# A scan over the running decay product, one add-and-clip per step, with matmuls on quadrants of TensorE

## The chip, the cores and the metric

The kernel runs on one core of a Trainium2 chip. Its time is the device time of a run in microseconds, from the first to the last instruction on the core, and the figure quoted is the median of several runs. Everything is computed in float32.

The engines that matter here are TensorE (PE, with its weight loads as PEld), VectorE (DVE), ScalarE (ACT) and GpSimd (POOL). Each works through its own queue in order and waits for the others by semaphores.

## The reference

The input x has 32 sequences of 256 tokens with 256 channels. A state-space block comes first, then two layers of local attention and a gated feed-forward network, and x is added at the end. The change touches the state-space block alone. Its core, cut to what matters:

```python
xn = layernorm(silu(conv(x @ W_in.T + cond)))            # [b, t, 512]
Bm, Cm, dt = split(xn @ W_xproj.T, 3)                    # 16 states each
Ad = 1.0 - 0.01 * tanh(dt @ W_dt.T + b_dt) * tanh(A_log) # decay, [b, t, 16]
Bd = Bm * min(norm(xn), 1)

def step(h, (ad, bd, xt, ct)):                           # h: [b, 16, 512]
    h = clip(h * ad[:, :, None] + bd[:, :, None] * xt[:, None, :], -10, 10)
    return h, einsum('bd,bdh->bh', ct, h)                # y of this step

y = scan(step, 0) + D * xn
out = (y * silu(gate)) @ W_out.T
```

A step depends on the state that the step before it left, and the clip keeps the recurrence from being written as one linear scan.

## The kernel before

Eight sequences are scanned together (a group; there are four groups). The state h is one tile of 128 partitions, 8 sequences times 16 states, by 512 channels. Time runs in 16 blocks of 16 steps; 8 sequences times 16 steps are the 128 token rows of a block. A group goes through the convolution, the scan, and two layers of attention and feed-forward; nothing of one group overlaps much with the next.

The inner loop, with two matmuls on TensorE and two operations on VectorE in each step:

```python
nxt = prep(0)
for tb in range(NTB):                       # 16 blocks
    xn, lbs, ct, ad, sg = nxt
    if tb + 1 < NTB:
        nxt = prep(tb + 1)                  # for the next block
    y = ps_y.tile([P, DI], FP, ...)
    for t in range(TB):                     # 16 steps
        h, s = divmod(t, TH)
        if s == 0:
            put_c(h, ct)
        bx = ps_bx.tile([P, DI], FP, ...)   # Bd * x of this step
        nc.tensor.matmul(bx, lbs[h][:, s * P : (s + 1) * P], xn, start=True, stop=True)
        h_new = hp.tile([P, DI], FP, ...)
        nc.vector.scalar_tensor_tensor(     # h * ad + bx
            h_new, h_old, ad[:, t : t + 1], bx, ALU.mult, ALU.add)
        nc.vector.tensor_scalar(h_new, h_new, -CLIP, CLIP, ALU.max, ALU.min)
        nc.tensor.matmul(y, ly[h][:, s * P : (s + 1) * P], h_new,
                         start=(t == 0), stop=(t == TB - 1))
        h_old = h_new
    z = sp.tile([P, DI], FP, ...)
    nc.gpsimd.tensor_mul(z, xn, dskip_sb)
    nc.vector.tensor_add(z, z, y)
    nc.gpsimd.tensor_mul(z, z, sg)
    ...                                     # 4 transposes to tz, ACT copies them to zT;
    ...                                     # every fourth block W_out: 8 matmuls to po
```

The weights of the first matmul, `lb`, are 128 by 128 for each step, zero but for the eight rows of that step, so only 8 of its 128 rows contribute. The weights of the second, `ly`, hold C of that step in the eight columns of its tokens.

What `prep` does for the next block, in order, shortened to the operations and their engines:

```python
def prep(tb):
    # PE    4 transposes of xc -> tp_x
    # DVE   bn_stats, bn_aggr, + eps; POOL ** -0.5; DVE xn = (tp_x - mean) * rstd
    # POOL  xn *= lng, xn += lnb
    # ACT   sum of squares -> ss; DVE sc = min(ss, 1); POOL nrm = sc ** 0.5
    # PE    4 transposes -> tp_xn; ACT copies them to xnT
    # PE    pp = xnT @ W_xproj.T; DVE copies it to pr
    # PE    pd = transpose of dt; DVE dT; PE pd2 = dT @ W_dt
    # DVE   da = pd2 + b_dt; ACT tanh; DVE * a_row
    bd = ...                                # DVE, 128 x 16
    for h in range(2):                      # lb: 2 x [128, 1024] on POOL
        nc.gpsimd.tensor_mul(lb, bc(ident_tb[:, h * TH : (h + 1) * TH, :], 3, NS),
                             bc(bc(bd, 1, GB), 1, TH))
    # DVE   wide (twice); PE pc = C and dt * A by (sequence, state) rows
    nc.vector.tensor_copy(ct, pc[:, 0:TB])
    nc.vector.tensor_scalar_add(ad, pc[:, TB : 2 * TB], 1.0)
    # POOL  xt; PE gp = xt @ W_in (gate), 2 matmuls; ACT sg = silu(gp)
    return xn, lbs, ct, ad, sg

def put_c(h, ct):                           # DVE, into the diagonal of ly
    nc.vector.tensor_mul(diag, bc(ct[:, h * TH : (h + 1) * TH], 2, GB), bc(of_seq, 1, TH))
```

Of the kernel before, what the change touches and what calls it, by code (L numbers as in the profile page):

```python
# [7 lines left out]

FP = mybir.dt.float32
AF = mybir.ActivationFunctionType  # L10
# [4 lines left out]
P = 128  # L15
S = 256          # tokens of a sequence
DM = 256         # model width
KM = DM // P
DI = 512         # inner width of the state-space block
NC_ = DI // P  # L20
NS = 16          # states per channel
GB = 8           # sequences scanned together: GB * NS = 128 partitions
TB = P // GB     # time steps of a token tile: GB * TB = 128 partitions
NTB = S // TB
TH = TB // 2
# [3 lines left out]
W = 128          # attention window  # L29
# [8 lines left out]
def bc(ap, axis, n):  # L38
    """ap with a new axis of n equal entries (stride 0)."""
    ap = ap.unsqueeze(axis)  # L40
    shape = list(ap.shape)
    shape[axis] = n
    return ap.broadcast_to(shape)
# [3 lines left out]
def kernel(  # L47
    ctx: ExitStack,
    tc: tile.TileContext,
    xT,        # [P, KM, B, S]      x, channel-major  # L50
    condT,     # [P, NC_, B]
    w_inT,     # [P, KM, 2 * DI]
    w_conv,    # [P, NC_, TAPS]
    b_conv,    # [P, NC_]
    s_ln_g,    # [DI]
    s_ln_b,    # [DI]
    w_xT,      # [P, NC_, 3 * NS]
    w_dtT,     # [NS, NS]
    b_dt,      # [NS]
    a_log,     # [NS]  # L60
    d_skip,    # [DI]
    w_outT,    # [P, NC_, DM]
    wqkv,      # [P, L, KM, 3 * DI]
    qk_scale,  # [L, 2, DH]
    qk_scale_sw,  # [L, 2, DH]      the halves of a head swapped
    wo,        # [P, L, NC_, DM]
    f_ln_g,    # [P, L, KM]
    f_ln_b,    # [P, L, KM]
    w1,        # [P, L, KM, 2 * HID]
    b1,        # [P, L, 2, len(MCH)]  # L70
    w2,        # [P, L, len(MCH), DM]
    b2,        # [P, L, KM]
    rot_c,     # [P, NW, 2, DH]     rotary tables of positions
    rot_s,     # [P, NW, 2, DH]
    outT,      # [P, KM, B, S]
):
# [44 lines left out]
    # Token tiles have partition b * TB + t; the scan has partition b * NS + n.  # L121
    # of_seq[p, b] = (p // TB == b), of_step[p, t] = (p % TB == t)
    of_seq = const.tile([P, GB], FP, tag="of_seq", name="of_seq")
    nc.vector.tensor_reduce(of_seq, ident.rearrange("p (b t) -> p b t", b=GB), AX.X, ALU.add)
    of_step = const.tile([P, TB], FP, tag="of_step", name="of_step")
    nc.vector.tensor_reduce(of_step, ident.rearrange("p (b t) -> p t b", b=GB), AX.X, ALU.add)
    ident_tb = ident.rearrange("p (b t) -> p t b", b=GB)
# [6 lines left out]
    # 0.01 * A, A = -tanh(A_log)  # L134
# [4 lines left out]
    # Additive mask of a window's queries over the window before it and itself.  # L139
# [11 lines left out]
    # Rotary tables with the layer's q and k scales in them.  # L151
# [18 lines left out]
    # Transposed weights of the state read-out, two half tiles: zero but where the step is.  # L170
    ly = []
    for i in range(2):
        t = const.tile([P, TH * (P + 1)], FP, tag=f"ly{i}", name=f"ly{i}")
        nc.gpsimd.memset(t, 0.0)
        ly.append(t)

    def rsqrt(pool, src, n, name):
        """src ** -0.5, [P, n]."""
        r = pool.tile([P, n], FP, tag=f"{name}_r", name=f"{name}_r")
        nc.gpsimd.tensor_tensor(r, src, neg_half[:, 0:n], ALU.pow)  # L180
        return r

    def group_scan(g, xg, res):
        """x -> y of the state-space block, into res (channel-major, column 0 of each
        sequence zero)."""
        with ExitStack() as es:
            xcp = es.enter_context(tc.tile_pool(name=f"xc{g}", bufs=1, reuse_waits="tile"))
            # token tiles side by side: [channel, block of steps, sequence, step]
            xc = xcp.tile([P, NC_, NTB, GB, TB], FP, tag="xc", name=f"xc_{g}")

            with tc.tile_pool(name=f"cv{g}", bufs=2, reuse_waits="tile") as cv, tc.tile_pool(
                name=f"cvp{g}", bufs=4, space=PSUM, reuse_waits="tile"
            ) as cvp:
                for j in range(GB // 2):
                    for c in range(NC_):
# [22 lines left out]
                        for k in range(1, TAPS):  # L218
# [4 lines left out]
                        nc.scalar.activation(  # L223
                            xc[:, c, :, 2 * j : 2 * j + 2, :].rearrange("p n b t -> p b n t"),
                            acc.rearrange("p b (n t) -> p b n t", n=NTB),
                            AF.Silu,
                        )

            sp = es.enter_context(tc.tile_pool(name=f"sp{g}", bufs=2, reuse_waits="tile"))
            hp = es.enter_context(tc.tile_pool(name=f"hp{g}", bufs=3, reuse_waits="tile"))  # L230
# [3 lines left out]
                tc.tile_pool(name=f"pbx{g}", bufs=3, space=PSUM, reuse_waits="tile")  # L234
            )
            ps_y = es.enter_context(
                tc.tile_pool(name=f"py{g}", bufs=2, space=PSUM, reuse_waits="tile")
# [8 lines left out]
            def prep(tb):  # L246
                """What the scan of a block of steps needs."""
                ts_ = slice(tb * TB, (tb + 1) * TB)
                tp = ps_t.tile([P, DI], FP, tag="tp", name="tp_x")
                for c in range(NC_):  # L250
                    nc.tensor.transpose(
                        tp[:, c * P : (c + 1) * P],
                        xc[:, c, tb].rearrange("p b t -> p (b t)"),
                        ident,
                    )
# [14 lines left out]
                # min(|xn|, 1)  # L270
# [35 lines left out]
                bd = sm.tile([P, NS], FP, tag="bd", name="bd")  # L306
                nc.vector.tensor_scalar_mul(bd, pr[:, 0:NS], nrm)
                # lb[(b, t), t', b', n] = Bd[(b, t), n] where t' = t and b' = b
                lbs = []
                for h in range(2):  # L310
                    lb = sp.tile([P, TH, GB, NS], FP, tag="lb", name="lb", bufs=3)
                    nc.gpsimd.tensor_mul(  # L312
                        lb,
                        bc(ident_tb[:, h * TH : (h + 1) * TH, :], 3, NS),
                        bc(bc(bd, 1, GB), 1, TH),
                    )
                    lbs.append(lb.rearrange("p t b n -> p (t b n)"))

                # C and dt * A from rows (b, t) to rows (b, n)
                wide = sm.tile([P, 2, GB, NS], FP, tag="wide", name="wide", bufs=1)  # L320
                nc.vector.tensor_mul(
                    wide[:, 0], bc(of_seq, 2, NS), bc(pr[:, NS : 2 * NS], 1, GB)
                )
                nc.vector.tensor_mul(wide[:, 1], bc(of_seq, 2, NS), bc(da, 1, GB))
                pc = ps_s.tile([P, DI], FP, tag="pss", name="pc")
                for i in range(2):
# [3 lines left out]
                        of_step,  # L330
# [3 lines left out]
                ct = sm.tile([P, TB], FP, tag="ct", name="ct")  # L334
                nc.vector.tensor_copy(ct, pc[:, 0:TB])
                ad = sm.tile([P, TB], FP, tag="ad", name="ad")
                nc.vector.tensor_scalar_add(ad, pc[:, TB : 2 * TB], 1.0)

                # silu(gate)
                xt = sm.tile([P, KM, GB, TB], FP, tag="xt", name="xt", bufs=2)  # L340
                nc.gpsimd.tensor_copy(xt, xg[:, :, :, ts_])
                gp = ps_t.tile([P, DI], FP, tag="tp", name="gp")
                for k in range(KM):
                    nc.tensor.matmul(  # L344
                        gp, xt[:, k].rearrange("p b t -> p (b t)"), w_in_sb[:, k, DI : 2 * DI],
# [4 lines left out]
                return xn, lbs, ct, ad, sg  # L350

            def put_c(h, ct):
                """ly[(b, n), s, (b', t')] = C[(b, n), t'] where t' = h * TH + s and b' = b"""
                diag = ly[h].rearrange("p (s r) -> p s r", r=P + 1)[
                    :, :, h * TH : h * TH + (GB - 1) * TB + 1 : TB
                ]
                nc.vector.tensor_mul(
                    diag, bc(ct[:, h * TH : (h + 1) * TH], 2, GB), bc(of_seq, 1, TH)
                )

            zT = None
            h_old = hp.tile([P, DI], FP, tag="h", name="h0")
            nc.vector.memset(h_old, 0.0)
            nxt = prep(0)
            for tb in range(NTB):
                xn, lbs, ct, ad, sg = nxt
                if tb + 1 < NTB:
                    nxt = prep(tb + 1)
                y = ps_y.tile([P, DI], FP, tag="y", name="y")
                for t in range(TB):  # L370
                    h, s = divmod(t, TH)
                    if s == 0:
                        put_c(h, ct)
                    bx = ps_bx.tile([P, DI], FP, tag="bx", name="bx")
                    nc.tensor.matmul(  # L375
                        bx, lbs[h][:, s * P : (s + 1) * P], xn, start=True, stop=True
                    )
                    h_new = hp.tile([P, DI], FP, tag="h", name="h")
                    nc.vector.scalar_tensor_tensor(  # L379
                        h_new, h_old, ad[:, t : t + 1], bx, ALU.mult, ALU.add  # L380
                    )
                    nc.vector.tensor_scalar(h_new, h_new, -CLIP, CLIP, ALU.max, ALU.min)  # L382
                    nc.tensor.matmul(  # L383
                        y, ly[h][:, s * P : (s + 1) * P], h_new,
                        start=(t == 0), stop=(t == TB - 1),
                    )
                    h_old = h_new

                # (y + D * xn) * silu(gate), then W_out
# [10 lines left out]
                if q == 0:  # L400
                    zT = zp.tile([P, NC_, 4, P], FP, tag="zT", name="zT")
                nc.scalar.copy(zT[:, :, q, :], tz.rearrange("p (c t) -> p c t", c=NC_))  # L402
# [376 lines left out]
```

## Time and profile before

Three runs took 7459.3, 7441.64 and 7459.2 us, median 7459.2. The profiled run:

| what | value |
|---|---|
| span | 7442.3 us |
| PE busy | 6294.6 us (85%) |
| PE weight loads | 3214.0 us (43%) |
| DVE busy | 3504.5 us (47%) |
| ACT busy | 1552.8 us (21%) |
| POOL busy | 1871.4 us (25%) |
| mean TensorE clock granted | 0.874 |

A group of instructions on the page is read so: source line, engine, operation, output and inputs, shape and count; then busy time in us and the mean of one in ns; then the idle time of the engine just before these instructions, and what ended it. PE busy times overlap at the ends of matmuls, so that starts, not durations, tell the rate. A line of the timeline gives the start, the duration, the engine, the source line, what was done and how often, and in brackets how long the engine had been idle and for whom.

### The profile page before, as it was taken

To read this page: it belongs to the slowest core of one execution; us is meant where nothing else is said; L and a number is where in the kernel's file an instruction comes from. 1 tells how busy PE (TensorE), PEld (TensorE's weight loads), DVE (VectorE), ACT (ScalarE), POOL (GpSimd) and SP (SyncE) were. 2 spreads that over 40 slices of the span, in tenths; PEclk is the share of its full clock that TensorE was granted. 3 is DMA by queue.
4 is the path that set the end of the run, shared out by engine and by line. 5 is a ranking of instruction groups with operands and counts; after the bars stand their busy time and mean duration, and the time that the engine had idled before them with its cause. 6 is when DMAs were issued, how large, how long until landed. Compare 5 with 4: busy or idle time off the path is not lost. (4 is left out here: it accounts for less than half of the span.)

```text
span 7442.3 us, 55547 instructions
## 1 busy us (share of the span) xinstructions
PE 6294.6 (85%) x19648; PEld 3214.0 (43%) x19648; DVE 3504.5 (47%) x6691; ACT 1552.8 (21%) x4066; POOL 1871.4 (25%) x1649
## 2 busy tenths in 40 slices
PE   6989888888799988888879898888887899888888
PEld 2444553553344455355334445535533444553553
DVE  5666442442566644244256664424425666442442
ACT  1000331331100033133110003313311000331331
POOL 3222330330322233033032223303303222330331
PEclk8999888888899988888889998888888999888888
DMA  2000000000000000000000000000000000000000
GB/s 74 0 0 12 1 1 0 1 6 14 3 0 0 12 1 1 0 1 6 15 3 0 0 12 1 1 0 1 6 16 2 1 0 0 1 0 0 1 6 17
DMA packets 14021, 40.37 MB, mean 5 GB/s; under 512 B 2352, under 2 KB 3376, under 8 KB 12080
## 3 DMA queue, kind: packets, MB, share of 16 engines
q1 hardware_dynamic: 10832, 34.78, 1.3%
q8 instruction: 156, 2.56, 0.1%
q10 hardware_dynamic: 2912, 2.05, 0.1%
q14 instruction: 121, 0.99, 0.0%
HBM read 28.43 MB, written 8.39 MB: 5 GB/s over the span
## 5 line engine op out<-in xcount | busy, mean ns | idle before, releaser
L383 PE MATMUL y<-h,ly 128*128 128x512 f32 x2048 | 1088.4, 616 | 83.4 <-DVE h L382 83.4
L375 PE MATMUL bx<-xn,lb 128*128 128x512 f32 x2048 | 1019.0, 596 | 3.0 <-POOL lb L312 3.0
L379 DVE SCALAR_TENSOR_TENSOR h<-h,ad,bx 128x512 f32<-128x512 f32 x1024 | 764.8, 747 | 392.8 <-PE bx L375 368.9
L180 POOL TENSOR_TENSOR ss_r<-ss,neg_half 128x8 f32<-128x8 f32 x256 | 420.2, 1641 | 1783.0 <-DVE ss L464 1773.7
L447 PE MATMUL ps_qkv<-wqkv_sb,res 128*128 128x512 f32 x1536 | 730.2, 597 | 0.0
L383 PEld LDWEIGHTS y<-h,ly 128*128 128x128 f32 x2048 | 375.7, 196 | 535.2 <-DVE h L382 420.2
L503 PE MATMUL sc<-kT,qT 64*128 64x128 f32 (+1 forms) x2048 | 578.3, 425 | 27.0 <-ACT kT L485 27.0
L375 PEld LDWEIGHTS bx<-xn,lb 128*128 128x128 f32 x2048 | 381.6, 190 | 445.6 <-issue 442.2
L382 DVE TENSOR_SCALAR h<-h 128x512 f32<-128x512 f32 x1024 | 557.9, 545 | 29.1
L511 DVE TENSOR_TENSOR p_sb<-sc,mask 128x512 f32<-128x512 f32 x384 | 257.7, 682 | 584.6 <-PE sc L503 433.6
L533 PEld LDWEIGHTS ov<-v_sb,pT 128*128 128x128 f32 x3072 | 479.1, 240 | 110.5 <-issue 41.5
L533 PE MATMUL ov<-v_sb,pT 128*128 128x64 f32 x3072 | 503.9, 326 | 8.8 <-DVE pT L530 7.1
L519 ACT ACTIVATE p_sb<-p_sb,nmax 128x128 f32<-128x128 f32 (+1 forms) x1024 | 453.5, 445 | 202.2 <-DVE nmax L515 198.4
L480 PE MATMUL tr_qk<-ident,rot 128*128 128x128 f32 x1024 | 181.7, 304 | 369.0 <-POOL rot L477 362.1
L624 PE MATMUL pg<-hT,w_sb 128*128 128x512 f32 (+1 forms) x768 | 420.9, 676 | 7.3 <-ACT hT L610 4.4
L635 DVE SCALAR_TENSOR_TENSOR ag<-pa,b_sb,gl 128x512 f32<-128x512 f32 x192 | 143.9, 750 | 577.5 <-PE pa L624 562.1
L402 ACT COPY zT<-tz 128x512 f32<-128x512 f32 x64 | 37.5, 585 | 1704.5 <-PE tz L396 1704.5
L180 POOL TENSOR_TENSOR ve_r<-ve,neg_half 128x1 f32<-128x1 f32 x192 | 105.5, 549 | 1135.5 <-DVE ve L599 1005.6
L312 POOL TENSOR_TENSOR lb<-ident,bd 128x1024 f32<-128x1024 f32 x128 | 258.0, 2017 | 522.5 <-PE bx L375 329.4
L503 PEld LDWEIGHTS sc<-kT,qT 64*128 64x128 f32 x2048 | 303.7, 219 | 191.5 <-ACT kT L485 90.2
L393 POOL TENSOR_TENSOR z<-z,sg 128x512 f32<-128x512 f32 x64 | 80.9, 1265 | 1170.2 <-DVE z L392 1170.2
L624 PE MATMUL pa<-hT,w_sb 128*128 128x512 f32 (+1 forms) x768 | 366.3, 599 | 0.0
(122 smaller groups left out, 8025.4 us busy)
## 6 DMA issues: line engine op xcount, KB each, us to landing
xg<-in_xT_dram SPq DMA_DIRECT2D x8, 1024.0 KB, 6.6
xs<-in_xT_dram SPq DMA_DIRECT2D x16, 512.0 KB, 4.0
out_dram<-fo SPq DMA_DIRECT2D x32, 256.0 KB, 2.0
wqkv_sb<-in_wqkv_dram SPq DMA_DIRECT2D x1, 3072.0 KB, 12.2
w_sb<-in_w_dram SPq DMA_DIRECT2D x1, 2728.0 KB, 12.2
w_sb<-in_w_dram SPq DMA_DIRECT2D x1, 1536.0 KB, 16.0
w_in_sb<-in_w_inT_dram SPq DMA_DIRECT2D x1, 1024.0 KB, 5.1
wo_sb<-in_wo_dram SPq DMA_DIRECT2D x1, 1024.0 KB, 4.9
```

Source lines behind the costliest of these rows:

```text
L180: nc.gpsimd.tensor_tensor(r, src, neg_half[:, 0:n], ALU.pow)
L312: nc.gpsimd.tensor_mul(lb, bc(ident_tb[:, h * TH : (h + 1) * TH, :], 3, NS), bc(bc(bd, 1, GB), 1, TH),)
L375: nc.tensor.matmul(bx, lbs[h][:, s * P : (s + 1) * P], xn, start=True, stop=True)
L379: nc.vector.scalar_tensor_tensor(h_new, h_old, ad[:, t : t + 1], bx, ALU.mult, ALU.add)
L382: nc.vector.tensor_scalar(h_new, h_new, -CLIP, CLIP, ALU.max, ALU.min)
L383: nc.tensor.matmul(y, ly[h][:, s * P : (s + 1) * P], h_new, start=(t == 0), stop=(t == TB - 1),)
L447: nc.tensor.matmul(ps, res[:, k, b, t0 : t0 + W], wqkv_sb[:, l, k, a * DI : (a + 1) * DI], start=(k == 0), stop=(k == KM - 1),)
L503: nc.tensor.matmul(sc[:, i, :], qT[rows, h0 + i, w * W : (w + 1) * W], kT[rows, h0 + i, k0 : k0 + nk], start=True, stop=True,)
L511: nc.vector.tensor_add(p_sb, sc, bc(mask[:, 2 * W - nk :], 1, nh))
L519: nc.scalar.activation(p_sb[:, i, :], p_sb[:, i, :], AF.Exp, bias=nmax[:, h : h + 1], accum_out=rsum[:, h : h + 1],)
L533: nc.tensor.matmul(ov[:, h, :], pT[:, i, kb * W : (kb + 1) * W], v_sb[:, k0 // W + kb, h * DH : (h + 1) * DH], start=(kb == 0), stop=(kb = ...
L624: nc.tensor.matmul(ps[0:n, :], w1_sb[:, l, k, half_ * HID + o : half_ * HID + o + n], hT[:, k].rearrange("p b t -> p (b t)"), start=(k == ...
```

## The change

With p[t] the product of all decays up to step t, the state over it, g = h / p, follows g[t] = clip(g[t-1] + (Bd x)[t] / p[t], -10 / p[t], 10 / p[t]). The multiplication by the decay leaves the inner loop: Bd is divided by p and C multiplied by p when a block is prepared, the limits become one value for each row and step, and add and clip can be one instruction of VectorE, a custom operation `TENSOR_ADD_SAT` (in0 + in1, then min with s0 and max with s1).

The tokens of a block are put in another order, (q, i, b) with step 4 i + q, so that a step's eight rows lie within one of four strips of 32 rows. The first matmul of a step then takes 32 rows of weights and of xn instead of 128, and the second writes 32 output rows instead of 128 (32 columns of weights). Four steps in turn use the four strips; each bx strip has a PSUM bank of its own.

What it is for: half the VectorE instructions in a step, and matmuls that need a quarter of the array, which four of them might share. The diff, cut to its core:

```diff
-            def prep(tb):
+            def prep(tb, p_old):
 ...
-                bd = sm.tile([P, NS], FP, tag="bd", name="bd")
-                nc.vector.tensor_scalar_mul(bd, pr[:, 0:NS], nrm)
-                lbs = []
-                for h in range(2):
-                    lb = sp.tile([P, TH, GB, NS], FP, tag="lb", name="lb", bufs=3)
-                    nc.gpsimd.tensor_mul(lb, ...)
 ...
-                nc.vector.tensor_copy(ct, pc[:, 0:TB])
                 nc.vector.tensor_scalar_add(ad, pc[:, TB : 2 * TB], 1.0)
+                nc.vector.tensor_tensor_scan(pd_, ad, zero_tb, p_old, ALU.mult, ALU.add)
+                nc.vector.reciprocal(pi, pd_)
+                nc.gpsimd.tensor_scalar_mul(lim[:, 0], pi, CLIP)
+                nc.gpsimd.tensor_scalar_mul(lim[:, 1], pi, -CLIP)
+                nc.vector.tensor_mul(ct, pc[:, 0:TB], pd_)
+                nc.gpsimd.tensor_mul(piw, ...)                # 128 x 128
+                nc.tensor.matmul(pp2[:, 0:NS], piw..., st_n, start=True, stop=True)
+                nc.vector.scalar_tensor_tensor(               # Bd / p
+                    bd, pr[:, 0:NS], nrm, pp2[:, 0:NS], ALU.mult, ALU.mult)
+                lb = sp.tile([P, NI * GB, NS], FP, tag="lb", name="lb", bufs=2)
+                nc.gpsimd.tensor_mul(lb, bc(tok_row, 2, NS), bc(bd, 1, NI * GB))
 ...
-                nc.vector.tensor_mul(                         # put_c
-                    diag, bc(ct[:, h * TH : (h + 1) * TH], 2, GB), bc(of_seq, 1, TH)
-                )
+                nc.gpsimd.tensor_mul(                         # put_c, once a block
+                    diag, bc(ct..., 3, GB), bc(bc(st_seq, 1, NQ), 1, NI))
 ...
+                put_c(lyt, ct)
-                for t in range(TB):
-                    ...                                       # the loop shown above
+                for i in range(NI):                           # 4 rounds
+                    hs = []
+                    for q in range(NQ):                       # of 4 steps
+                        t = i * NQ + q
+                        rows = slice(32 * q, 32 * q + 32)
+                        bx = ps_bx.tile([P, DI], FP, tag=f"bx{q}", name=f"bx{q}")
+                        nc.tensor.matmul(
+                            bx, lb[rows, i * GB : (i + 1) * GB, :]..., xn[rows, :],
+                            start=True, stop=True)
+                        h_new = hp.tile([P, DI], FP, tag="h", name="h")
+                        nc.vector._custom_dve(
+                            TENSOR_ADD_SAT, out=h_new, in0=h_old, in1=bx,
+                            s0=lim[:, 0, t : t + 1], s1=lim[:, 1, t : t + 1])
+                        hs.append(h_new)
+                        h_old = h_new
+                    for q in range(NQ):
+                        t = i * NQ + q
+                        nc.tensor.matmul(
+                            y[32 * q : 32 * q + 32, :], lyt[:, 32 * t : 32 * t + 32],
+                            hs[q], start=(i == 0), stop=(i == NI - 1))
```

Cut here: comments, the constants, the new order of tokens in xc, xt (two copies on POOL in place of one) and in the copies of the output, and the SiLU after the convolution, which becomes two instructions of 256 elements in place of one of 512. The buffers of h grow from 3 to 8; bx has four banks with one buffer each in place of three buffers; y has one buffer in place of two.

## The prediction

> **What bounds the kernel now.** I read four views in this order: the page's slices and groups (where the time is), the busy time by stretch (what the scan is worth), the timeline of one block of 16 steps (what waits for what), and the order of both programs' instructions on each engine. First the page: the rows of slices (tenths busy, and the clock), and the groups of the scan.
>
> ```profile
> PE   6989888888799988888879898888887899888888
> DVE  5666442442566644244256664424425666442442
> PEclk8999888888899988888889998888888999888888
> ...
> L383 PE MATMUL y<-h,ly 128*128 128x512 f32 x2048 | 1088.4, 616 | 83.4 <-DVE h L382 83.4
> L375 PE MATMUL bx<-xn,lb 128*128 128x512 f32 x2048 | 1019.0, 596 | 3.0 <-POOL lb L312 3.0
> L379 DVE SCALAR_TENSOR_TENSOR h<-h,ad,bx 128x512 f32<-128x512 f32 x1024 | 764.8, 747 | 392.8 <-PE bx L375 368.9
> ...
> L382 DVE TENSOR_SCALAR h<-h 128x512 f32<-128x512 f32 x1024 | 557.9, 545 | 29.1
> ```
>
> The pattern repeats four times (four groups of 8 sequences); the "666" and the clock digits "999" mark the scan. One f32 matmul leaves two records (2048 for 1024), so one step costs TensorE two matmuls and VectorE two operations. Two of the four scans by stretch:
>
> ```profile
> 1930.00:2600.00 670.00, 603.52 (x1580) 278.61 (x1581) 409.78 (x785) 47.76 (x104) 170.25 (x144) 0.94 0.01 4
> ...
> 5645.00:6315.00 670.00, 604.82 (x1583) 279.22 (x1584) 409.74 (x785) 48.34 (x105) 169.39 (x142) 0.94 0.00 0
> ```
>
> The columns are length, then busy time of PE, PE loads, DVE, ACT, POOL, then clock. A scan takes about 670 us, so the four take 2680 of 7442 us; PE is busy 90% of it, DVE 61%. The steady part of a block (timeline of PE, then of DVE):
>
> ```profile
> 5939.56 1.02 PE L375 MATMUL bx<-xn,lb 128*128 128x512 f32 x2
> 5940.42 1.02 PE L383 MATMUL y<-h,ly 128*128 128x512 f32 x2
> 5941.28 1.02 PE L375 MATMUL bx<-xn,lb 128*128 128x512 f32 x2
> ```
>
> ```profile
> 5938.91 0.75 DVE L379 SCALAR_TENSOR_TENSOR h<-h,ad,bx 128x512 f32<-128x512 f32 x1 [0.51 <-PE bx L375]
> 5939.69 0.43 DVE L382 TENSOR_SCALAR h<-h 128x512 f32<-128x512 f32 x1
> 5940.62 0.75 DVE L379 SCALAR_TENSOR_TENSOR h<-h,ad,bx 128x512 f32<-128x512 f32 x1 [0.51 <-PE bx L375]
> ```
>
> Starts of matmuls are 0.86 us apart without a gap; DVE idles 0.51 us in each step for bx. The step is 1.72 us, all TensorE: 16 steps are 27.5 us. Yet blocks follow each other every 41.8 us (the DVE clip that waits behind POOL recurs at 5756.81, 5797.99, 5842.59 and 5883.51). The other 14 us come from preparing the next block, whose chain is threaded into the same queues:
>
> ```profile
> 5952.12 0.75 PE L280 MATMUL tp_xn<-ident,xn 128*128 128x128 f32 x4 [1.98 <-POOL xn L268]
> 5952.87 2.08 PE L344 MATMUL gp<-w_in_sb,xt 128*128 128x512 f32 x2
> ...
> 5956.56 0.21 DVE L293 COPY pr<-pp 128x48 f32<-128x48 f32 x1 [2.37 <-PE pp L288]
> ...
> 5958.61 0.28 DVE L298 COPY dT<-pd 16x128 f32<-16x128 f32 x1 [1.17 <-PE pd L296]
> ...
> 5960.25 0.17 DVE L302 TENSOR_TENSOR da<-pd,bdt_sb 128x16 f32<-128x16 f32 x1 [1.36 <-PE pd L300]
> ```
>
> PE idles 1.98 us for POOL's layer norm, then DVE waits in turn for pp, pd, pd and pc; from 5952 to 5963 only one step is added. The stretch 5952 to 5963 has a clock of 0.69, so its matmuls are slower (gp: 2.08 us for two records).
>
> [...] idle time of 1.98 us is followed by the clock of 0.69. [...] the clip L382 takes 0.43 us alone and 1.97 us while POOL writes lb (2.02 us).
>
> **The change, part by part.**
> - *VectorE.* Multiply-add (0.75) and clip (0.43) become one add with limits. It has L379's shape and one PSUM input, so I give it 0.75, 0.78 from start to start. A block's 16 steps: 12.5 us in place of 18.9. The plain clip was what stalled behind POOL, so some 1.5 us a block of that go too. New: scan, reciprocal, both on 128x16, about 0.25 each, partly for ct's copy. put_c (two of 0.60) goes to POOL. DVE was not the bound, so none of this counts by itself.
> - *POOL.* lb shrinks from two of 2.02 us to one 128x512, about 1.1; limits, piw and put_c add about 1.5. Hidden, but piw now lies between DVE's reciprocal and PE's pp2.
> - *TensorE.* The same 32 matmuls a block, each still 512 columns and two records of 0.43, now on quadrants. [...] I do not expect four in the time of one, but a new matmul each 0.43 us: (4+1) x 0.43 = 2.15 us for four in place of 3.44.
> - *Order.* The built program's PE order in a steady round of four steps is y0 y1 y2, next bx0, y3, next bx1 bx2 bx3. y takes column strips and bx row strips of the whole array[...].
>
> A steady round, from the end of the last add (0): y2 ends 0.08, bx0 runs 0.18 to 1.04, y3 1.1 to 2.0, bx1 2.1 to 2.96; 0.2 us later (3.2) DVE starts three adds of 0.78 and ends at 5.5. bx2 and bx3 come 0.43 apart and are in time. So 5.5 us for four steps (1.38 a step) against 6.9.
>
> One whole block by the built order: round 0 ends its adds at 5.5; z (0.68, then POOL 1.27) lets PE transpose at 4.3, tp_x ends at 5.4. Four y to 7.6, four bx to 9.9. Meanwhile st to xn on DVE end at 8.3 and POOL's two xn at 11.1; round 1 adds until 11.1, the last after sc at 12.9. tp_xn, ACT, gp, pp, gp at half clock: pr at 15.5, gp to 17.1, pd, dT 17.8, one y, pd2, da, tanh, wide 20.4. The other y and bx0 let round 2 start at 22.2; with bx1 to bx3 it ends at 26.3. Reciprocal 26.6, POOL's lim and piw 27.3, pp2 at 27.4 in front of y3: y3 to 28.4, bx1 29.4, adds 29.6 to 31.9. So 32 us against 41.0; the W_out product (6.95 us, every fourth block) now sits in front of the remaining y, adding about 1.3 a block on average, against 0.8 now. 33.3 against 41.8 is 8.5 saved, x 64 blocks = 544 us.
> - *Convolution.* SiLU in two halves costs ACT about 0.3 more per tile of 64; the chain there is POOL and DVE, so at most part shows: +12 us.
> - Sum: 7459 - 544 + 12 = 6927.
>
> **Rivals.**
> - *No concurrency in f32.* 64-row score matmuls exist already, but consecutive ones share their rows, so the trace says nothing. Then 32 x 0.86 = 27.5 + about 6.5 of preparation at full clock + 1.5 idle + 1 to 2 of switches = 37: still better than 41.8, as eight matmuls now stand in front of tp_xn and cover POOL's latency. Time 7459 - 64 x 4.8 = about 7150.
> - *Half clock.* If quarter-used strips count as little activity, or the new waits (pp2, tp_xn) idle PE too long, bx0, y3 and bx1 take 1.72 each: 7.9 us a round and about 47 us a block, 7800. [...] Against: in the steady round PE has hardly a gap.
> - *Full concurrency.* Four in 0.86 us: the round stays at 5.5, since the three dependent matmuls y2/bx0, y3, bx1 and three adds are the chain; only the bursts shrink, to about 31 a block: 6800.
> - *A slow custom add.* 0.25 us more each is about 0.75 a round, 3 a block: 7120.
>
> **Range and chances.** The main path gives 6927, full concurrency 6800, no concurrency 7150, half clock 7800. I lean a little upwards, to 6960, range 6700 to 7320. Faster by over 2% (under 7310): 0.84; within: 0.08; slower: 0.08, nearly all of it the half clock.
>
> **What would show it.** The groups bx and y keep 2048 records each; their starts in a burst 0.43 apart confirm half overlap, 0.86 none, under 0.25 full. The new add near 0.75, and DVE's idle time moving to waits for bx after y3, in a stretch of about 540 us per scan; POOL's 1.97 stalls gone; attention unchanged. A scan clock well under 0.9, or adds over 0.9 us, would prove me wrong.

## The result, and the profile after

The changed kernel takes 7242.7 us (median of 4 runs, 7238.7 to 7244.4) against 7459.3 before: a ratio of 0.972, with a 95% interval of 0.971 to 0.974. It is faster, by 217 us, where 499 were expected.

First the page of the changed kernel: its rows of slices, and the groups of the scan (out<-in, partitions x elements, count | busy us, mean ns of one | idle time of the engine before them, and its releaser).

```profile
PE   6988888888788888888878888888887888888888
DVE  4444442442444444244244444424424444442442
PEclk8778878888877887888888788798887778879878
...
L421 DVE CUSTOM_DVE_ANT_0 h<-h,bx,lim 128x512 f32<-128x512 f32 x1024 | 825.4, 806 | 759.9 <-PE bx L413 705.3
L429 PE MATMUL y<-h,ly 128*32 128x512 f32 x2048 | 857.1, 766 | 10.6 <-DVE h L421 10.6
L413 PE MATMUL bx<-xn,lb 32*128 32x512 f32 x2048 | 733.2, 782 | 0.0
```

VectorE has fallen to 4 tenths in the scans, as meant, and now waits for bx (705 of its 760 us of idle time at this line). But the clock digits of the scans have gone from 9 to 7 and 8, and a record of y or bx shows 770 ns on average where it showed 600, although each matmul uses a quarter of the array. The same in one window of the second group, from the z of its first block to the z of its last (length, then busy time of PE, PE loads, DVE, ACT, POOL, then the clock):

```profile
1944.00:2492.00 548.00, 484.04 (x1474) 153.97 (x1472) 256.19 (x479) 41.97 (x91) 131.78 (x184) 0.78 0.01 4
```

TensorE is busy for 88% of it, much as before, at a clock of 0.78 in place of 0.94. The timeline of TensorE shows a stretch of a block at half clock (0.50 from 5605.0 to 5611.4), and after it one at full clock (1.00 from 5614.5 to 5625.0):

```profile
5605.05 2.07 PE L413 MATMUL bx<-xn,lb 32*128 32x512 f32 x2
5607.05 0.61 PE L355 MATMUL pp<-st_n,piw 128*128 128x16 f32 x2
5607.59 1.92 PE L429 MATMUL y<-h,ly 128*32 128x512 f32 x2
5609.43 2.08 PE L413 MATMUL bx<-xn,lb 32*128 32x512 f32 x6
5611.44 3.17 PE L429 MATMUL y<-h,ly 128*32 128x512 f32 x6
5614.55 1.12 PE L413 MATMUL bx<-xn,lb 32*128 32x512 f32 x2
...
5619.85 1.68 PE L429 MATMUL y<-h,ly 128*32 128x512 f32 x8
5621.46 1.14 PE L413 MATMUL bx<-xn,lb 32*128 32x512 f32 x8
```

The order is the one foreseen: bx0, y3 (one matmul, two records), bx1 to bx3, y0 to y2, bx0. (In every block two of the four joints between rounds have all four y and then all four bx instead, as in the last two lines.) In the first lines a single matmul lasts 1.9 to 2.1 us, and bx0 to the next bx0 is 9.5 us. In the last line, at full clock, eight records, that is four matmuls on four strips, lie within 1.14 us. The timeline of VectorE in the same stretch:

```profile
5607.16 0.81 DVE L421 CUSTOM_DVE_ANT_0 h<-h,bx,lim 128x512 f32<-128x512 f32 x1 [2.87 <-PE bx L413]
...
5611.54 2.70 DVE L421 CUSTOM_DVE_ANT_0 h<-h,bx,lim 128x512 f32<-128x512 f32 x3 [3.44 <-PE bx L413]
```

Three adds in a row take 2.70 us, so they start (2.70 - 0.81) / 2 = 0.94 us apart, and before them VectorE waits 3.4 us for bx1, which stands behind y3 at half clock.

Where the 206 us between the two profiled spans come from (7442.3 and 7236.7; sums over the four groups, between marks in both traces: first bn_stats, z of the first and last block, last QKV product):

```
                                          before    after
convolution, up to the first bn_stats      966.0    986.6    +20.6
first block, bn_stats to z                 211.3    214.8     +3.5
the other 60 blocks, z to z               2446.1   2194.3   -251.8
last z to the last QKV product            3579.6   3602.0    +22.4
```

A block takes 36.6 us on average in place of 40.8: 4.2 saved, where 8.5 were expected.

### The profile page after: what moved, and what is told of

Its sections match the earlier page's. It is cut to its first block, busy times and chain, and to the rows that moved or that the text cites. A ratio compares the mean times of both kernels' runs of the same rounds, so it can differ in the third digit from the quotient of the medians.

```text
span 7236.7 us, 55107 instructions
## 1 busy us (share of the span) xinstructions
PE 6051.1 (84%) x19776; PEld 2809.3 (39%) x19776; DVE 2972.4 (41%) x5670; ACT 1582.7 (22%) x4134; POOL 1775.1 (25%) x1906
## 5 line engine op out<-in xcount | busy, mean ns | idle before, releaser
L421 DVE CUSTOM_DVE_ANT_0 h<-h,bx,lim 128x512 f32<-128x512 f32 x1024 | 825.4, 806 | 759.9 <-PE bx L413 705.3
L429 PE MATMUL y<-h,ly 128*32 128x512 f32 x2048 | 857.1, 766 | 10.6 <-DVE h L421 10.6
L413 PE MATMUL bx<-xn,lb 32*128 32x512 f32 x2048 | 733.2, 782 | 0.0
L578 PE MATMUL tr_p<-ident,p_sb 128*128 128x128 f32 x1536 | 358.6, 348 | 4.4 <-ACT p_sb L569 4.4
L413 PEld LDWEIGHTS bx<-xn,lb 32*128 32x128 f32 x2048 | 188.3, 218 | 442.6 <-issue 439.0
L692 PE MATMUL po_f<-ag,w_sb 128*128 128x512 f32 (+1 forms) x768 | 356.9, 609 | 0.0
L497 PEld LDWEIGHTS ps_qkv<-wqkv_sb,res 128*128 128x128 f32 x1536 | 264.9, 191 | 211.4 <-issue 211.4
L526 POOL TENSOR_TENSOR rot<-rot,swp 128x512 f32<-128x512 f32 x256 | 324.7, 1268 | 69.7 <-DVE swp L523 69.7
```

What stands on the lines that cost most here:

```text
L413: nc.tensor.matmul(bx, lb[rows, i * GB : (i + 1) * GB, :].rearrange("p b n -> p (b n)"), xn[rows, :], start=True, stop=True,)
L421: nc.vector._custom_dve(TENSOR_ADD_SAT, out=h_new, in0=h_old, in1=bx, s0=lim[:, 0, t : t + 1], s1=lim[:, 1, t : t + 1],)
L429: nc.tensor.matmul(y[32 * q : 32 * q + 32, :], lyt[:, 32 * t : 32 * t + 32], hs[q], start=(i == 0), stop=(i == NI - 1),)
L497: nc.tensor.matmul(ps, res[:, k, b, t0 : t0 + W], wqkv_sb[:, l, k, a * DI : (a + 1) * DI], start=(k == 0), stop=(k == KM - 1),)
L526: nc.gpsimd.tensor_add(rot, rot, swp)
L578: nc.tensor.transpose(tr[:, i, ks], p_sb[:, i, ks], ident)
```

## The experiments

The theory after the result was this: the rounds are as quick as foreseen when the clock is full, but bx on 32 rows lets the clock fall, and everything in the half-clock stretches takes nearly twice as long (a bx 2.07 us in place of 1.12). Rivals: the longer add (0.94 us from start to start, not 0.78); no real concurrency of f32 matmuls in strips; the order of y and bx in the queue, with its switches between row strips and column strips; and the idle time of TensorE, which alone might lower the clock. Every kernel below was compared with the kernel before on its own chip (7447 to 7451 us there); "clock" is that of the 60 blocks between z and z.

### m1_streams: TensorE alone

The whole computation is left out. What remains are streams of f32 matmuls of 512 columns without any waits between them, each after 24 matmuls on the whole array:

```diff
-    for g in range(NG): group_scan(...), attention(...), feed_forward(...)
+    64 x  matmul(bk[j % 4], w0, mv(j))                        # L743 whole array
+    64 x  matmul(bk[0], w0[0:32, :], mv(j)[0:32, :])          # L746 one strip of 32 rows
+    256 x matmul(bk[q], w0[rs(q), :], mv(j)[rs(q), :])        # L750 four row strips in turn
+    64 x  matmul(bk[j % 4][0:32, :], w0[:, 0:32], mv(j))      # L753 one strip of 32 columns
+    256 x matmul(bk[..][rs(q), :], w0[:, rs(q)], mv(j))       # L757 four column strips in turn
+    32 x  (4 row strips, 4 column strips)                     # L761, L763
+    32 x  (1 row strip, 1 column strip)                       # L766, L767
+    64 x  matmul(bk[0], w0[0:64, :], mv(j)[0:64, :])          # L770 64 rows
```

> Only streams of f32 matmuls, 512 columns each, with no waits between them, ten stretches in a row: whole array, one 32-row strip, four row strips in turn, one 32-column strip, four column strips in turn, bursts of four row strips and four column strips, one row strip and one column strip by turns, 64 rows; 24 whole-array matmuls ahead of each. Theory A [...]: the stretches with one strip fall to clock 0.5, so a matmul takes 1.71 us there; whole array and four strips stay at 1.0. Theory B (only idle time of TensorE lowers the clock): every stretch stays at 1.0, a single strip 0.86 us a matmul. Both: four strips in about 1.0 us a burst, since the changed kernel's bursts of four follow at that distance; row by turns with column about 1.0 a matmul at full clock.

Its timeline of TensorE (start, length, records), the 24 matmuls of L739 between the streams left out:

```profile
37.88 55.10 PE L743 MATMUL b<-xg,w_in_sb 128*128 128x512 f32 x128
...
113.51 104.43 PE L746 MATMUL b<-xg,w_in_sb 32*128 32x512 f32 x128
...
240.29 55.22 PE L750 MATMUL b<-xg,w_in_sb 32*128 32x512 f32 x512
...
316.23 55.12 PE L753 MATMUL b<-xg,w_in_sb 128*32 128x512 f32 x128
...
392.08 55.14 PE L757 MATMUL b<-xg,w_in_sb 128*32 128x512 f32 x512
...
467.95 1.14 PE L761 MATMUL b<-xg,w_in_sb 32*128 32x512 f32 x8
469.02 1.06 PE L763 MATMUL b<-xg,w_in_sb 128*32 128x512 f32 x8
470.01 1.14 PE L761 MATMUL b<-xg,w_in_sb 32*128 32x512 f32 x8
...
640.53 55.20 PE L770 MATMUL b<-xg,w_in_sb 64*128 64x512 f32 x128
```

And two windows of it, one within L743, one within L746:

```profile
44.00:92.00 48.00, 48.00 (x114) 21.21 (x113) 0.00 (x0) 0.00 (x0) 0.00 (x0) 1.00 0.00 0
120.00:217.00 97.00, 97.00 (x115) 37.63 (x113) 0.00 (x0) 0.00 (x0) 0.00 (x0) 0.50 0.00 0
```

Three readings. Four strips, of rows or of columns, do 512 records in the 55.1 us in which the whole array does 128: full concurrency, in f32 too, and the rival without it falls. A lone strip of 32 rows is never idle, and yet its clock is 0.50 (from 5 us after its start until 3 us after its end), with 128 records in 104 us. A lone strip of 32 columns has 1.00 (320 to 370), and so have four row strips at once (245 to 295) and the alternating bursts (470 to 530); 64 rows take as long as the whole array (55.20 us for 128 records against 55.10 at 1.00), and the stream that alternates one row strip and one column strip shows no half clock (1.12 and 1.05 us a matmul). So time in use alone does not set the granted clock: with TensorE never idle it was 0.50 for a stream on 32 rows and 1.00 for one on all rows; the number of rows in use counts, and 32 columns in place of 128 made no difference. The expectation that one strip of either kind halves the clock was right for rows alone. Last, eight records of four strips recur every 1.03 us where rows and columns alternate (467.95, 469.02, 470.01: 2.06 for two), against 4 x 0.214 = 0.86 without alternation: a switch costs 0.17 us. Single matmuls of the two kinds by turns start 1.01 us apart, against 0.86 for a column strip alone: a row strip and a column strip did not run side by side.

### e1, e3, e4: the quadrants of bx and of y, each undone alone

e3 gives bx all 128 rows again, with zeros in lb outside the strip of the step; e4 gives y all 128 columns again; e1 does both, so that of the main change the add with limits, the preparation over p and the rounds of four remain. The number of h buffers falls from 8 to 5, 6 and 3 (e3, e4, e1) for space, and lb in e3 and e1 takes GpSimd four products a block in place of one. The order on TensorE and VectorE is that of the changed kernel in e3, but not in e1 and e4: there the four bx and then the four y of a round follow each other throughout.

```diff
-   bx, lb[rows, i * GB : (i + 1) * GB, :], xn[rows, :]       # e3, e1: all rows
+   bx, lb[i // 2][:, q, (i % 2) * GB : (i % 2 + 1) * GB, :], xn
-   y[32 * q : 32 * q + 32, :], lyt[:, 32 * t : 32 * t + 32], hs[q], start=(i == 0)
+   y, ly[i // 2][:, P * (t % 8) : P * (t % 8) + P], hs[q], start=(t == 0)   # e4, e1: all columns
```

> The changed kernel with the quadrants taken back: same states over the decay product and same fused add, but every matmul of a step on all 128 rows and 128 columns (weights zero outside the step's rows), as before. Theory A: clock back at about 0.94 in the scan, step bound by two matmuls of 0.86, block 37 to 38 us, time 7130 to 7230, so no slower than the changed kernel although it does four times the array work. Theory B: the clock in the scan stays near 0.78, as the waits for POOL are the same, and the time is 7450 or more.

> The changed kernel with bx alone taken back to all 128 rows; y stays on column strips. Theory A: a bx alone in the queue costs the same as a strip, a burst of four 3.44 instead of 1.0, but the clock rises to over 0.85: time within 100 us of the changed kernel, 7150 to 7340. Theory B: clock as in the changed kernel, about 10 us more a block: 7500 or more.

> The mirror of the last experiment: the changed kernel with bx on 32-row strips, but y back on all 128 columns of weights, so a round's four y cost 3.44 us in place of 1.0. Theory A, as it stands after the streams (the gate counts the rows that work, columns do not matter[...]): rows in use in a round about 78%, clock 0.95 or more, block 29 to 32 us, time 6800 to 6980. Rival A2 (any 32-row strip in the scan pulls the clock down, however much else runs): clock below 0.85 and time over 7250.

Measured, with the changed kernel as the fourth cell:

```
us (ratio to before, interval)         clock   mean block
bx, y whole           e1  7327.9 (0.982 to 0.985)   0.98   38.4
bx strips, y whole    e4  7273.1 (0.975 to 0.978)   0.91   37.1
bx whole, y strips    e3  6840.1 (0.917 to 0.920)   1.00   30.2
bx strips, y strips       7242.7 (0.971 to 0.974)   0.78   36.6
```

The same window of e3's second group, and its two groups of matmuls:

```profile
1840.00:2294.00 454.00, 442.47 (x1475) 170.29 (x1473) 256.75 (x479) 41.88 (x91) 174.22 (x226) 1.00 0.01 5
```

```profile
L426 PE MATMUL bx<-xn,lb 128*128 128x512 f32 x2048 | 1019.3, 620 | 0.0
L442 PE MATMUL y<-h,ly 128*32 128x512 f32 x2048 | 539.1, 605 | 0.0
```

Here is the main finding. e3 takes all concurrency away from bx, so TensorE has more to do (four bx in 3.44 us, not in about 1), and it is 403 us faster than the changed kernel. The clock is 1.00 throughout; VectorE, its adds (806 ns) and the order are the same. So neither the longer add nor the order cost the expected gain: with both unchanged, a block takes 30.2 us, less than the 33.3 of the prediction. The theory for e3 had foreseen a higher clock, but only 7150 to 7340 us.

The row strips of bx save 55 us where y is whole and cost 403 where y is on strips. From e1 to e3 the column strips of y bring 488 us, together with the change of order named above. Without any strips, e1 is 120 us under the kernel before on its own chip (7447.7), which is less than 2%; its theory, 7130 to 7230, was missed although the clock came back. e4 missed its forecast of 6800 to 6980: the clock rose to 0.91 only, and y in series stands in the chain between two adds. Its y and its next bx at full clock:

```profile
2059.16 3.96 PE L435 MATMUL y<-h,ly 128*128 128x512 f32 x8 [0.88 <-DVE h L427]
2063.05 1.14 PE L419 MATMUL bx<-xn,lb 32*128 32x512 f32 x8
```

### e5: bx on strips of 64 rows

```diff
-   rows = slice(32 * q, 32 * q + 32)
+   rows = slice(64 * (q // 2), 64 * (q // 2) + 64)     # lb twice as large, zeros in the other half
```

> The changed kernel with bx on two strips of 64 rows in place of four of 32 (weights of two steps side by side, zero outside their rows), everything else as it is. A burst of four then takes 1.7 to 2.6 us in place of 1.0. Theory A: a lone 64-row matmul kept the full clock in the streams, so the clock is over 0.93 and the block 28 to 31 us: 6740 to 6900. Rival B2 (what helped with all rows was the longer bursts, which fill TensorE's idle time, not the rows): clock and time stay halfway, 6950 to 7150.

7096.2 us (0.951 to 0.954), clock 0.90, 33.5 us a block. With 32, 64 and 128 rows in the same order the clock is 0.78, 0.90, 1.00 and the time 7243, 7096, 6840. It did not reach the forecast of 6740 to 6900: 64 rows held the full clock in a stream without pauses (m1, 55.20 us for 128 records), but not in the blocks here, which have waits (0.90). The result lies in the rival's range of time (6950 to 7150), so this run alone does not tell rows in use from TensorE's idle time; for that see e2 and e6 below.

### e7: the add with limits in two operations

```diff
-   nc.vector._custom_dve(TENSOR_ADD_SAT, out=h_new, in0=h_old, in1=bx, s0=lim.., s1=lim..)
+   nc.vector.tensor_add(h_new, h_old, bx)
+   nc.vector.tensor_scalar(h_new, h_new, lim.., lim.., ALU.min, ALU.max)
```

> The changed kernel with the fused add taken apart: an add, then a clip with the two limits, so a step costs VectorE about 1.2 us in place of 0.94. If the adds between the last bx of a round and the next y lie on the path (three a round): 0.3 x 3 x 4 = 3 to 4 us a block more, 7420 to 7500. If TensorE at half clock hides them: under 7300.

7278.6 us (0.975 to 0.980): 36 us slower than the changed kernel. (The profiled execution is the slowest of the four, 7306.3 us.) The two operations take 685 and 590 ns where the one took 806:

```profile
L421 DVE TENSOR_TENSOR h<-h,bx 128x512 f32<-128x512 f32 x1024 | 701.0, 685 | 261.5 <-PE bx L413 221.0
L422 DVE TENSOR_SCALAR h<-h,lim 128x512 f32<-128x512 f32 x1024 | 603.8, 590 | 20.1
```

Some 480 us more of VectorE's time cost 36. But the blocks after the first are quicker than those of the changed kernel (35.8 us), at a higher clock (0.93 in three of the groups, 0.85 in one), and the loss lies in the first block of each group (84 to 86 us from bn_stats to z, against 54), where other instructions came in front. The order of y and bx in the queue changed too, to runs of one to three, and TensorE idles for 5% of the 60 blocks in place of 12%. So the 36 us do not measure the length of the add, and the forecast under 7300 was met for a reason other than the one written: the clock rose. Why it is higher with the same strips was not separated. That the add is not what cost the gain rests on e3 alone.

### e2, e6, e8: y of a round behind bx of the next

In the changed kernel y3 stands between bx0 and bx1, waits for the last add, and holds up bx1. Here the four y of a round stand behind the four bx of the next round:

```diff
     for i in range(NI):
         ... four bx, four adds
-        four y of this round
+        if pend is not None: y_round(pend)       # four y of the round before, then z when it is the last
+        pend = (i, hs, y, lyt, ...)
```

e2 does that alone, e6 with bx on 64-row strips (issued as steps 0, 2, 1, 3, so that neighbours lie on different strips), e8 with bx on all rows. The buffers of h are 8, 7 and 5 (7 in e5 too).

> The changed kernel with the read-out matmuls of a round queued behind the four bx matmuls of the next round, so that y of the last step no longer stands between the adds of two rounds, and y always comes as four strips at once. Theory A: three or two bursts a round in place of four, the round falls from 5.5 to about 4 us at full clock, share of the array in use rises from about 31% to over 40%, the clock rises above 0.85: block 29 to 31 us, time 6700 to 6850. Theory B: the clock stays at 0.78 or falls, since TensorE now idles more: block 34 to 36, time 6950 to 7080. A third theory (the preparation chain, not the rounds, sets the block): under 60 us gained, 7180 to 7240.

> 64-row strips together with y queued behind the next round's bx. Theory A: full clock and the short round add up: three bursts of about 1.0, 0.9 and 0.9 us against four adds of 0.94, so VectorE sets the round at about 3.8 us and the block comes to 24 to 27 us: 6450 to 6650. Rival (the preparation chain, about 14 us from the layer norm to the decay, bounds the block whatever the rounds do): the block stays at 28 to 29, 6720 to 6800.

> The fourth cell of a square: order of y as changed (7243) or late (6808), rows of bx 32 (clock 0.78) or all 128 (6840, clock 1.00); here both, late y and all rows. If the order and the clock acted one beside the other, the gains would add: 6843 x 6808 / 7243 or so, 6400 to 6450. My theory: the clock returns to 1.00, but TensorE then has 4 x (3.44 + 1.03) = 17.9 us of scan matmuls in a block and some 5 of preparation, and the chain of the preparation stands at about 26, so 6580 to 6720, with blocks of 26 to 27 us without W_out. Rival: only the length of the burst of bx counts once y is late; then 3.44 us of bx in a row is worse than two strips of 64 rows and it ends over 6760.

```
rows of bx        32            64            128
y as changed      7242.7 0.78   7096.2 0.90   6840.1 1.00     us, clock
y late            6807.6 0.78   6707.0 0.94   6609.5 1.00
ratios of the second row: 0.912 to 0.916, 0.899 to 0.902, 0.886 to 0.889
```

The windows of the second group, e2, then e6, then e8:

```profile
1840.00:2281.00 441.00, 395.70 (x1459) 151.25 (x1460) 253.41 (x472) 41.17 (x91) 128.83 (x183) 0.79 0.01 5
```

```profile
1812.00:2230.00 418.00, 355.93 (x1461) 137.04 (x1458) 252.10 (x470) 39.16 (x88) 140.12 (x180) 0.93 0.02 6
```

```profile
1782.00:2178.00 396.00, 386.23 (x1462) 149.04 (x1462) 256.00 (x474) 39.61 (x91) 171.38 (x225) 1.00 0.02 6
```

The order is worth 435 us at 32 rows with the clock unchanged, and 231 at 128 rows; the rows are worth 403 and 198. They are two separate causes that overlap: with either repaired, less is left for the other. e2 came in at the time of its theory A (6700 to 6850), but not for all of its reasons: the clock was to rise above 0.85 and stayed at 0.78.

e2 and e6 speak against the rival of idle time. They have the same order of y and bx, and in e6 TensorE idles longer (62 of 418 us in the window, against 45 of 441), yet with 64 rows in place of 32 its clock is 0.93 in place of 0.79. (Part of the difference in idle time may be an effect of the clock: a bx that takes 2.07 us in place of 1.12, as in the changed kernel, leaves less of a pause. m1 has no pause: 32 rows at 0.50, 64 in the time of the whole array.) Nor are rows the only thing that counts: e7 has the strips of the changed kernel, less idle time (5% against 12%) and a higher clock (0.85 to 0.93 against 0.78).

The order has two effects, which no run separates: y3 no longer stands in front of bx1, and the four y always run together. At 128 rows nearly all of its worth is TensorE's own time. From e3 to e8 the window is 58.0 us shorter, TensorE's busy time in it 56.2 and its idle time only 1.8. In e3 a y alone takes 1.04 us and three together 1.25; the four of e8 take 1.06 (below). From the timeline of e3:

```profile
2019.61 1.25 PE L442 MATMUL y<-h,ly 128*32 128x512 f32 x6
2020.78 1.12 PE L426 MATMUL bx<-xn,lb 128*128 128x512 f32 x2
2021.84 1.04 PE L442 MATMUL y<-h,ly 128*32 128x512 f32 x2
```

In e8 TensorE is busy for 97.5% of the window, as in e3, but of a shorter window. Its timeline in one block:

```profile
2013.78 1.06 PE L466 MATMUL y<-h,ly 128*32 128x512 f32 x8
2014.78 1.13 PE L491 MATMUL bx<-xn,lb 128*128 128x512 f32 x2
2015.74 0.27 PE L264 MATMUL tp_x<-ident,xc 128*128 128x128 f32 x1
2015.85 2.90 PE L491 MATMUL bx<-xn,lb 128*128 128x512 f32 x6
2018.68 1.06 PE L466 MATMUL y<-h,ly 128*32 128x512 f32 x8
```

Four bx in series, four y in 1.06 us, no gap: 4.9 us a round, with one transpose of the preparation in it. TensorE is the bound again, now at full clock. The expectation for e8, 6580 to 6720, held, with blocks of 25.4 us without W_out where 26 to 27 were written; e6 lay between its theory and its rival.

### e9, e10, e11: W_out elsewhere, the layer norm on VectorE

e9 is e6 with the two halves of the W_out product behind y in rounds 1 and 2 of the next block. e10 is e9 with `nc.gpsimd.tensor_mul(xn, xn, lng_sb)` and `tensor_add(xn, xn, lnb_sb)` on `nc.vector`; e11 is e8 with these two.

> The version with 64-row strips and late y (6707), with the W_out product moved: each of its two halves of 3.5 us stands behind y in rounds 1 and 2 of the next block, in place of both in a row behind z. There every fourth block was 34.6 against 27.2 us. If TensorE's idle time takes it in, 12 of the 16 products (the last of each group stays at the end) save up to 7 us each, 84 in all: 6620 to 6660, and the blocks all 27 to 30. Rival: queues are in order, so each half holds up the preparation's products or bx just as before: 6690 to 6720.

> As the run before, and the two products of the layer norm on xn go from POOL (1.27 us each) to VectorE (about 0.65 each). If the preparation's chain sets the block, 1.2 us less in it is worth 64 x 1.2 = 77 us: 6540 to 6590. Rival: the scan's adds, which wait on VectorE meanwhile, are pushed back by as much, and the time stays within 25 us of the run before, or rises.

> The version with all rows for bx and late y (6609, clock 1.00, blocks of 25.4 us), and the two layer-norm products on xn on VectorE. With strips of 64 rows that step was worth 104 us, at a clock that moved meanwhile. Here the clock should stay at 1.00, so the step is read cleanly: if the chain through xn sets the block, 1.2 to 1.6 us each, 6500 to 6540. Rival: TensorE, with 17.9 us of scan matmuls and some 5 of preparation in 25.4, is itself near the bound, so less than half of it shows: 6570 to 6610.

e9: 6745.6 us (0.903 to 0.907), slower than e6 by 39, so its theory falls and even its rival (6690 to 6720) was too low; the block with W_out still takes some 6 us more than its neighbours (33.5 against 27.4), and the clock of the 60 blocks is 0.92 where e6 has 0.94. e10: 6641.8 (0.890 to 0.895), 104 less than e9, more than the whole 77 of its theory. e11: 6607.0 (0.886 to 0.890), within 3 us of e8: its rival was right. In e11 TensorE is busy for 98.7% of the window:

```profile
1782.00:2177.00 395.00, 389.73 (x1455) 152.23 (x1454) 257.58 (x496) 39.30 (x88) 138.39 (x198) 1.00 0.02 6
```

The same edit is worth 104 us where TensorE idles at a moving clock, and nothing clear of noise where TensorE is the bound. The best versions are e8 and e11, 11% under the kernel before and nearly 9% under the changed kernel.

## Why the prediction was wrong

The direction was right and the size was not. The time lies inside the stated range of 6700 to 7320, but in its upper part, where the prediction had put the rivals without concurrency (7150) and with a slow add (7120). Neither came true; the slow clock put the time there, so the range held by luck. By its steps:

- *The fused add: 0.75, 0.78 from start to start.* Too short: 0.81, and 0.94 from start to start. The three adds in a round's chain thus take 2.70 us where about 2.3 were reckoned. That this did not cost the gain is shown by e3, which has the same adds and blocks of 30.2 us.
- *"A new matmul each 0.43 us: (4+1) x 0.43 = 2.15".* Wrong: four matmuls on four strips take about 1.0 us, in the kernel (1.14 for eight records) and in m1 (1.03 with switches, 0.86 without). So the rival of full concurrency came true in the bursts, and this error hid part of the one in the adds. Against four matmuls on the whole array (3.44 us) that is 4.0 times as fast without switches and 3.3 times with them.
- *The order of a round, and 5.5 us for it.* The order was right. Sorting the rounds by the clock within them (start of the first add of a round to that of the next; medians), those wholly at full clock take 7.15, 9.94, 5.75 and 6.53 us for rounds 0 to 3, together 29.4; the prediction's walk through a block gave 32.
- *W_out: +1.3 a block on average.* Right: round 0 at full clock is 8.70 on average against its median of 7.15, so 1.55. With it a block at full clock would be 30.9 us, where 33.3 were predicted.
- *Half clock in the preparation stretch alone.* This is the step that failed. Of the rounds, only 17 of 56 (round 1), 5 of 56 (round 2) and 6 of 56 (round 3) were at full clock throughout; the others took 13.3, 8.5 and 8.6 us (medians). The walk has half clock from tp_xn to pr and full clock everywhere else. All rounds together average 8.7, 12.1, 8.1 and 8.7, that is 37.6 a block against the 30.9 of full clock; over the 56 blocks sorted so (14 of each group) the missing clock cost an estimated 6.7 x 56 = 375 us. Without it the time would be near 6870, against the walk's 6927. Few rounds of this kernel were at full clock, but in e3 all are (8.8, 10.0, 5.5 and 6.5 on average, also 30.7 a block), and it measured 6840.
- *8.5 us "x 64 blocks".* Only 60 of the 64 are intervals between blocks, and those saved 4.2 us each; the first block of each group saved nothing (214.8 us for the four, 211.3 before). At 8.5 us a block, the four that do not count are 34 us.
- *The half-clock rival.* It came nearest to the cause, "if quarter-used strips count as little activity" (in m1 a lone strip of 32 rows has 0.50, one of 32 columns 1.00), and got a chance of about 0.08 because PE has "hardly a gap in the steady round". That argument takes the busy share for what sets the clock; m1's lone strip of rows has no gap at all and runs at 0.50. The rival's size was too large in turn: it took half clock for the whole scan (47 us a block), while in the trace half and full clock alternate within a block.
- *The convolution: +12.* +20.6, and about the same (20.4 to 21.6) in e1, e3, e6, e7 and e8: it goes with the new layout and the split SiLU, not with the scan. Which of the two it is was not tried.
- *Attention unchanged.* The stretch up to the last QKV product grew by 22 us in the changed kernel and by 1 us in e1. Its cause was not tried.
- *POOL's stalls gone* and *VectorE waiting for bx after y3*: right; no add takes longer than 0.81 us, and the timeline shows the wait of 3.44 us. *A scan of about 540 us*: 548 from the first z to the last plus 54 for the first block, so about 600. *"A scan clock well under 0.9, or adds over 0.9 us, would prove me wrong"*: the clock came, at 0.78; an add took 0.81, and only the distance from start to start is over 0.9.

What stays open is what sets the granted clock. In the trace before, waits of one length are followed by both: after 1.98 us for POOL's layer norm (to 5952.12) gp takes 2.08 us, and after 1.99 us in the next block 1.12:

```profile
6000.94 0.66 PE L280 MATMUL tp_xn<-ident,xn 128*128 128x128 f32 x4 [1.99 <-POOL xn L268]
6001.69 1.12 PE L344 MATMUL gp<-w_in_sb,xt 128*128 128x512 f32 x2
```

So already there the idle time just before a matmul did not settle its clock. The runs add that rows in use count (m1: 0.50 on 32 rows, never idle). But why 64 rows keep the full clock in that stream and have 0.90 in e5, why e4 has 0.91, and why e7 has 0.93 in three groups with the strips of the changed kernel, no run shows.

## What to carry to other kernels

Before splitting a matmul over strips, ask what each strip does to the clock: splitting output columns left it at 1.00 here (e3), while filling unused rows with zeros, which is more work, was 403 us faster, in a kernel where TensorE is near the bound and often runs one strip at a time. Then look at the order in the queue: keep the matmuls on different strips together, since one alone takes the time of four (a y in e3 1.04 us, four in e8 1.06), and do not let one that waits for the newest result stand in front of one that the next result needs (which of the two counts for more, the runs at 32 rows do not tell). And an edit's worth holds for the bound it was measured under: the layer norm on VectorE was worth 104 us in one version and 3 in another.

## What the runs showed of the hardware that was not expected

- Matmuls on a lone strip of 32 rows, back to back, run at a clock of 0.50 (816 ns a record over 104.4 us); a strip of 32 columns at 1.00 (430 ns), and 64 rows in the same 430 ns.
- Four strips of 32 rows or of 32 columns run f32 matmuls fully side by side: 108 ns a record against 430 for the whole array.
- Alternating bursts of row strips and column strips cost 0.17 us a switch (1.03 us for four matmuls in place of 0.86); single matmuls that alternate start 1.01 us apart in place of 0.86.
- The add with limits takes 0.81 us for 128x512 with one operand in PSUM, and 0.94 from start to start when each depends on the one before.
